# First loads reordered, a third q/k buffer and a VectorE norm for the last two tiles, in a linear-attention and FP4 feed-forward block

## The chip, the cores and the metric

The program runs on one core of one Trainium2 chip. The metric is the device time in microseconds (us) of one execution; for the kernel before, three runs gave 818.48, 820.93 and 820.97 us, so the median is 820.93 us. Lower is better. One further execution was recorded by the hardware profiler; all traces quoted here come from that one.

## What is computed

The input is x of shape (16, 512, 256). It goes through one transformer block, cut here to what matters:

```python
q, k = favor(split_heads(x @ Wq + bq)), favor(split_heads(x @ Wk + bk))   # softmax over 16 elements
v = split_heads(x @ Wv + bv)                                              # 16 heads of 16
attn = (q @ k.T / (sum(q) + EPS)) @ v @ Wo + bo
x = layernorm(x + attn)
h = silu(fp4(x) @ fp4(w_gate).T) * (fp4(x) @ fp4(w_up).T)                 # 704 wide
x = layernorm(x + fp4(h) @ fp4(w_down).T)
```

`fp4` quantises in blocks of 16 elements to the E2M1 grid with one scale a block and gives back f32 values. All matmuls are f32. The kernel uses that (q k^T) v equals q (k^T v), so no 512 x 512 matrix is formed.

## The kernel before, in words

The 16 batches have four tiles of 128 rows each; two tiles make a pair, so there are 32 pairs. For a batch, `load_x` (L373) brings x in one 512 KB DMA on SP's queue; `project` (L709), once a pair, transposes x on TensorE (`transposed`, L610, tile xT, copied out of PSUM by ScalarE at L620), multiplies by Wq and Wk (L724) and Wv (L734), adds the biases on VectorE (L727, L740), takes group maxima (L746) and subtracts them on GpSimd (L750). `features` (L754), once a batch, does exp on ScalarE (L761), sums on VectorE (L763), reciprocals (L774) and the scaling on GpSimd (L780). `key_values` (L784) forms k^T v (L793), masks it and multiplies by Wo (L807) into M. `attend` (L819), once a pair, transposes q (L617), multiplies by M (L835), and calls `norm`; the result x1n is written to DRAM.

`quantise` (L850), once a pair, reads x1 back from DRAM (L853, on SP's queue), finds FP4 codes (`codes`, L623: L635, L639 to L648), transposes them by a DMA (L864), spreads the scales by a PE transpose and a way through DRAM (L657 to L666), and multiplies both on GpSimd (L869) into xqT. `gate_up` (L873) does 32 matmul instructions of 352 columns (L889), SiLU (L894), the product (L896), FP4 codes again, a transposing DMA (L928) and the product on GpSimd (L932). `down` (L936) does 24 matmul instructions of 256 columns (L946), and `norm` with x1 as the residual; y goes out on ScalarE's queue (L957). For the last pair `down` calls `norm` for each tile by itself (L953), so that `us` holds one tile.

`norm` (L670): VectorE adds the residual and accumulates the row sum (L678); ScalarE takes the negative mean (L685) and the sum of squares (L687); GpSimd works out variance, the power -0.5 and the shift (L691 to L693); ScalarE applies them (L700).

The FFN's weights are quantised by the exact form of FP4 on the chip itself, in 8 chunks for gate and up and 4 for down (`weight_scales` L467, `fp4_exact` L506): some eight VectorE instructions a chunk, after one reduction over the whole of the raw weights (L477) and a row of scale arithmetic (L491 to L501). Their transposes (L562, L600) must be done before the first gate_up and the first down.

What sets the order: every piece of work is an `op` with an engine, an estimated time, a due time and its inputs and outputs. `Plan.order` (L145) is a list scheduler run on the host: over and over it takes, of each engine, the op that can start earliest (within 0.02 us the one due first), with the estimated end of its inputs plus 0.3 us, and the buffer that it needs must be free. The instructions are written out in that order, and each engine and DMA queue then runs its own in order on the chip. The estimates of the first loads are part of this: `DMA:x0` 6.0 us, `wqkv` 7.0, `wo` 14.0, `wgu` 13.0, `wdn` 16.0 (L377, L418 to L421). A `buf(shape, tag, n, name)` is one of n rotating buffers; an op that needs the n+1st waits until the first one's last reader is done. Counts that matter here: x 4 (L374), qk 2 (L713), v 2, x1 8 (`X1`, L315), x1n 3 (L842), xq 3 (L859, holds both xn and sqx).

The first loads are written out ahead of the plan in `load_all` (L425): x of batch 0 on SP's queue, then Wq, Wk, Wv on ScalarE's queue with bq, bk, bv on SP's, then w_gate, w_up and w_down, their big parts on ScalarE's queue (L440, L444) and two 64 KB tails on SP's (L443). SP follows with x of batch 1, then Wo and bo (`load_wo`, L446), and x of batches 2 and 3.

Of the kernel before, what the change touches and what calls it, by code (L numbers as in the profile page):

```python
# [13 lines left out]
ALU = mybir.AluOpType  # L14
AX = mybir.AxisListType

P = 128
# [11 lines left out]
LN_EPS = 1e-5  # L29
# [221 lines left out]
def t_dve(n):  # L251
    return 0.15 + n / 960.0
# [15 lines left out]
def tile_favor_fp4_block(  # L268
# [16 lines left out]
    nc = tc.nc  # L285
    B, L, D = hidden.shape
    FF = w_gate.shape[0]
    TPB = L // P
    PPB = TPB // 2
# [3 lines left out]
    D2, D3 = 2 * D, 3 * D  # L293
# [18 lines left out]

    NFF = 6

    X1 = 8  # L315
    plan = Plan()
    op = plan.op

    def buf(shape, tag, bufs, name, dtype=F32):
        return Buf(sb, [P] + list(shape), tag, bufs, name, dtype)  # L320
# [45 lines left out]
    def pu(ap):  # L366

        return ap.rearrange("p (u d) -> p u d", u=2)
# [3 lines left out]

    def load_x(b, due):  # L373
        x = buf([TPB, D], "x", 4, f"x_{b}")  # L374
        op("SP", 0.1, due, lambda: nc.sync.dma_start(x.tile, hidden[b].rearrange("(t p) d -> p t d", p=P)),
           outs=[x])
        op(f"DMA:x{b}" if b < 4 else "DMA", (6.0, 9.0, 16.0, 18.0, 3.5)[min(b, 4)], due, lambda: None, outs=[x])  # L377
        if b == 1:
            op("SP", 0.1, due, load_wo)
        xs[b] = x  # L380

    w_qkv = const.tile([P, DC, D3], F32, name="w_qkv")
# [1 line left out]
    w_o = const.tile([P, DC, D], F32, name="w_o")  # L384
    b_o = const.tile([P, D], F32, name="b_o")
    ident = const.tile([P, P], F32, name="ident")
    neg_half = const.tile([P, 2], F32, name="neg_half")
# [14 lines left out]
    gu_b, dn_b = big("wgu"), big("wdn")  # L402
    gu_flat = lambda: gu_b.tile.rearrange("p a b -> p (a b)")
    gu_rows = lambda: gu_flat().rearrange("p (c k) -> p c k", k=D)
    dn_flat = lambda: dn_b[:, 0, :]
    dn_rows = lambda: dn_flat().rearrange("p (c k) -> p c k", k=FF)
# [10 lines left out]

    wqkv_in, wo_in = (loaded(n, t) for n, t in (("wqkv", 7.0), ("wo", 14.0)))  # L418
    NGU, NDN = NW * D // F2, DC * FF // F2
    op("DMA:wgu", 13.0, 0.0, lambda: None, outs=[(gu_b, k) for k in range(NGU)])  # L420
    op("DMA:wdn", 16.0, 0.0, lambda: None, outs=[(dn_b, k) for k in range(NDN)])  # L421
    wguT_b = [Fixed(f"wguT{i}") for i in range(2)]
    wdT_b = Fixed("wdT")

    def load_all():  # L425

        gu_b.make()
        dn_b.make()
        gu_raw, dn_raw = gu_rows(), dn_rows()
        head = [o for o in plan.ops if o.eng == "SP"][:1]  # L430
        for o in head:
            for b in o.new:
                b.make()
            o.fn()
            o.fn = lambda: None
        for i, (w, bias) in enumerate(((Wq, bq), (Wk, bk), (Wv, bv))):
            nc.scalar.dma_start(w_qkv[:, :, i * D : (i + 1) * D], w.rearrange("(c p) n -> p c n", p=P))
            nc.sync.dma_start(b_qkv[:, i * D : (i + 1) * D], bias.partition_broadcast(P))
        for i, w in enumerate((w_gate, w_up)):
            nc.scalar.dma_start(  # L440
                gu_raw[:, i * NR : (i + 1) * NR, :], w[: NR * P].rearrange("(c p) k -> p c k", p=P)
            )
            nc.sync.dma_start(gu_raw[i * TR : (i + 1) * TR, 2 * NR, :], w[NR * P :])  # L443
        nc.scalar.dma_start(dn_raw, w_down.rearrange("(c p) k -> p c k", p=P))  # L444

    def load_wo():  # L446
        nc.sync.dma_start(w_o, Wo.rearrange("(c p) n -> p c n", p=P))
        nc.sync.dma_start(b_o, bo.partition_broadcast(P))

    def fill():  # L450
        make_identity(nc, ident)
# [218 lines left out]
    def norm(pr, add, dst, name, due, ins, r, junk, us=range(2)):  # L670

        n = len(us)
        key = None if n == 2 else us[0]
        rs, nm, var, rstd, nb = (buf([n], t if n == 2 else t + "1", 3, f"{t}_{name}") for t in ("rs", "nm", "var", "rstd", "nb"))

        def total():
            for k, u in enumerate(us):
                nc.vector.scalar_tensor_tensor(  # L678
                    r[:, u, :], pu(pr.tile)[:, u, :], 1.0, add(u), ALU.mult, ALU.add, accum_out=rs[:, k : k + 1]
                )  # L680

        op("DVE", n * (t_dve(D) + 0.06), due, total, ins=[(pr, key)] + ins, outs=[(r, key), rs])

        def square():
            nc.scalar.activation(nm.tile, rs.tile, AF.Identity, scale=-1.0 / D)  # L685
            for k, u in enumerate(us):
                nc.scalar.activation(junk(u), r[:, u, :], AF.Square, bias=nm[:, k : k + 1],  # L687
                                     accum_out=var[:, k : k + 1])

        def root():  # L690
            nc.gpsimd.tensor_scalar(var.tile, var.tile, 1.0 / D, LN_EPS, ALU.mult, ALU.add)  # L691
            nc.gpsimd.tensor_tensor(rstd.tile, var.tile, neg_half[:, :n], ALU.pow)
            nc.gpsimd.tensor_tensor(nb.tile, nm.tile, rstd.tile, ALU.mult)  # L693

        op("ACT", 0.35 + 0.6 * n, due, square, ins=[(r, key), rs], outs=[(dst, key), var, nm])
        op("POOL", 1.1, due, root, ins=[nm], outs=[var, rstd, nb])

        def apply():
            for k, u in enumerate(us):
                nc.scalar.activation(  # L700
                    dst[:, u, :], r[:, u, :], AF.Identity, bias=nb[:, k : k + 1], scale=rstd[:, k : k + 1]
                )

        op("ACT", 0.6 * n, due, apply, ins=[(r, key), nb, rstd], outs=[(dst, key)])


    qks, vs, Ms = {}, {}, {}

    def project(b, p, due):  # L709

        n = f"{b}_{p}"
        if p == 0:
            qks[b] = buf([TPB, D2], "qk", 2, f"qk_{b}")  # L713
            vs[b] = buf([TPB, D], "v", 2, f"v_{b}")
        x, qk, v = xs[b], qks[b], vs[b]
        xT = transposed(
            lambda: [x[:, 2 * p + u, c * P : (c + 1) * P] for u in range(2) for c in range(DC)],
            "xT", f"xT_{n}", due, [x],
        )
        for u in range(2):  # L720
            t = 2 * p + u
            pqk = psum("pm", f"pqk_{n}_{u}")
            for c in range(DC):
                op("PE", t_pe(D2), due, lambda c=c, u=u, pqk=pqk: nc.tensor.matmul(  # L724
                    pqk.tile, xT[:, 2 * u + c, :], w_qkv[:, c, :D2], start=c == 0, stop=c == DC - 1
                ), ins=[xT, wqkv_in], outs=[pqk], holds=[qk])
            op("DVE", t_dve(D2), due, lambda t=t, pqk=pqk: nc.vector.tensor_tensor(  # L727
                qk[:, t, :], pqk.tile, b_qkv[:, :D2], ALU.add), ins=[pqk], outs=[(qk, t)])
        pv = psum("pm", f"pv_{n}")

        def mm_v():
            for u in range(2):
                for c in range(DC):
                    nc.tensor.matmul(  # L734
                        pv[:, u * D : (u + 1) * D], xT[:, 2 * u + c, :], w_qkv[:, c, D2:],
                        start=c == 0, stop=c == DC - 1,
                    )

        op("PE", 2 * DC * t_pe(D), due, mm_v, ins=[xT, wqkv_in], outs=[pv], holds=[v])
        op("DVE", t_dve(2 * D), due, lambda: nc.vector.tensor_tensor(  # L740
            v[:, 2 * p : 2 * p + 2, :], pu(pv.tile), twice(b_qkv[:, D2:]), ALU.add
        ), ins=[pv], outs=[(v, p)])
        G = 2 * 2 * H
        mx = buf([G], "mx", 3, f"mx_{n}")
        qk3 = lambda: qk[:, 2 * p : 2 * p + 2, :].rearrange("p u (g e) -> p (u g) e", e=HD)
        op("DVE", t_dve(2 * D2), due, lambda: nc.vector.tensor_reduce(mx.tile, qk3(), AX.X, ALU.max),  # L746
           ins=[(qk, 2 * p), (qk, 2 * p + 1)], outs=[mx])
        for u in range(2):
            g = slice(u * 2 * H, (u + 1) * 2 * H)
            op("POOL", t_pool(D2), due, lambda g=g: nc.gpsimd.tensor_tensor(  # L750
                qk3()[:, g, :], qk3()[:, g, :], bcast(mx[:, g], HD), ALU.subtract
            ), ins=[mx], outs=[(qk, 2 * p + u)])
# [64 lines left out]
    st = {}  # L817

    def attend(b, p, due):  # L819
        i = b * PPB + p  # L820
        two = slice(2 * p, 2 * p + 2)
        x, qk, M = xs[b], qks[b], Ms[b]
# [6 lines left out]
           ins=[x, wo_in], outs=[xb])  # L829
# [9 lines left out]

        r = buf([2, D], "r1", 2, f"r1_{i}")  # L840
        op("PE", 2 * DC * t_pe(D), due, mm_a, ins=[qT, M], outs=[pa], holds=[r, xb], name="attend")
        x1 = buf([2, D], "x1n", 3, f"x1n_{i}")  # L842
        norm(pa, lambda u: xb[:, u, :], x1, f"a{i}", due, [xb], r, lambda u: x1[:, u, :])

        d = Buf(dr, [P, 2, D], "x1", NP, f"dx1_{i}")
# [4 lines left out]
    def quantise(i, due):  # L850
        x1 = st[i]["x1"] = buf([2, D], "x1", X1, f"x1_{i}")
        d = st[i]["d"]
# [3 lines left out]
        flat = lambda b: b.tile.rearrange("p u d -> p (u d)")  # L856
        am, iv = (small(n // BLK, t + "x", f"{t}_x{i}") for t in ("am", "iv"))
        scales = am, buf([n // BLK], "nsx", 2, f"ns_x{i}"), iv
        xn, sq = (buf([2, D], "xq", 3, f"{t}_{i}") for t in ("xn", "sqx"))  # L859
        xc = buf([n], "xc", 2, f"xc_{i}", U16)  # L860
        codes((lambda: flat(x1), x1), (lambda: flat(xn), xn), (lambda: flat(sq), sq), xc, 0, n, scales, 0,
              f"x{i}", due)
# [174 lines left out]
```

## Time and profile before

| what | value |
|---|---|
| median of three runs | 820.93 us |
| the profiled execution's own time | 821.11 us |
| its span, first to last instruction | 818.9 us |
| TensorE (PE) busy, matmul instructions | 786.8 us (96%), 3246 |
| VectorE (DVE) busy | 611.6 us (75%) |
| ScalarE (ACT) busy | 412.3 us (50%) |
| GpSimd (POOL) busy | 417.7 us (51%) |
| first matmul of the projections (L724) starts | 11.62 us |
| first gate_up matmul (L889) starts | 258.02 us |
| last matmul ends, last DMA issued | 812.6 us, 816.14 us |

The span is what lies between the first and the last instruction of the profiled execution; 2.2 us of its own time lie outside it. Engine rows count busy time; a busy TensorE can still run at half rate, so matmul counts times columns are the surer measure. In timeline rows the first number is the start in us, the second the length of the merged row, "x8" the number of instructions in it, and the bracket the idle time of that engine before the row with what ended it; ACTq and SPq are the DMA-issuing queues of ScalarE and SP.

### The profile page before, as it was taken

Reading aid. Unit: us, or ns where it says so; the run is one execution under the profiler, and the core shown is the slowest. Engines: PE = TensorE matmul, PEld = TensorE weight load, DVE = VectorE, ACT = ScalarE, POOL = GpSimd, SP = SyncE. Lnnn points to the kernel's source line nnn. Section 1 sums busy time; section 2 is a strip of 40 time slices with the busy share of each in tenths; the row PEclk is TensorE's granted clock in tenths of the full one; section 3 lists DMA queues with packets and bytes.
Section 4 is the critical chain, followed back from the end, with each engine's and each line's share of the span. In section 5 each row is a group of like instructions: output and inputs, shape, how many; then the busy total and the mean of one; then the engine's idle time right before and its main releaser. Section 6 shows DMA issues by size and latency. Waiting matters only on the chain.

```text
span 818.9 us, 10331 instructions
## 1 busy us (share of the span) xinstructions
PE 786.8 (96%) x3246; PEld 568.3 (69%) x3246; DVE 611.6 (75%) x1200; ACT 412.3 (50%) x924; POOL 417.7 (51%) x513
## 2 busy tenths in 40 slices
PE   5889998999999999999999999999999999999996
PEld 3566676767776767777777677777767777677674
DVE  1998998998888888668766765767767677675562
ACT  1245665745776563536563654544444444444433
POOL 0478786869888564536463534333333324333331
PEclk9989998999999999999999999999999999999999
DMA  8102241303012437766646564779797797886431
GB/s 280 32 0 93 89 146 31 109 2 104 27 38 79 88 65 150 124 100 107 112 102 100 106 123 115 127 147 144 123 148 135 145 141 131 147 131 126 119 76 38
DMA packets 104683, 85.98 MB, mean 105 GB/s; under 512 B 65037, under 2 KB 88117, under 8 KB 104629
## 3 DMA queue, kind: packets, MB, share of 16 engines
q1 hardware_dynamic: 84680, 63.81, 42.5%
q10 hardware_dynamic: 19949, 21.52, 9.4%
q8 instruction: 25, 0.41, 0.2%
q14 instruction: 29, 0.24, 0.1%
HBM read 51.25 MB, written 18.70 MB: 85 GB/s over the span
## 4 chain that ended last, share of the span: by engine, by line
PE 85%; DVE 8%; DMA 2%; POOL 2%; ACT 2%; issue 1%; SPq 0%; ACTq 0%; POOLq 0%; DVEq 0%
PE bank L889 36%; PE bank L946 20%; PE bank L724 11%; PE bank L835 6%; PE bank L734 5%; PE bank L793 3%; PE bank L617 2%; PE bank L807 2%; POOL qk L780 1%; DMA x<-dx 1%; DMA b_qkv<-in_L_attn_bk_dram 1%; DVE mx L746 1%; PE bank L657 1%; DVE qk L727 1%; DVE fs L763 1%
## 5 line engine op out<-in xcount | busy, mean ns | idle before, releaser
L889 PE MATMUL bank<-w_guT,xqT 128*128 128x352 f32 x1024 | 310.3, 459 | 0.0
L889 PEld LDWEIGHTS bank<-w_guT,xqT 128*128 128x128 f32 x1024 | 194.2, 190 | 101.4 <-issue 0.7
L946 PE MATMUL bank<-w_dT,hq 128*128 128x256 f32 x768 | 174.8, 380 | 0.6 <-DVE r L678 0.6
L932 POOL TENSOR_TENSOR hq<-hcT,hq 128x768 f32<-128x768 bf16 (+1 forms) x62 | 94.1, 1539 | 136.5 <-DMA hq<-d_h 117.3
L946 PEld LDWEIGHTS bank<-w_dT,hq 128*128 128x128 f32 x768 | 142.1, 190 | 24.9 <-issue 3.9
L896 DVE TENSOR_TENSOR h<-bank,g 128x352 f32<-128x352 f32 x128 | 66.3, 521 | 94.6 <-PE bank L889 53.9
L724 PE MATMUL bank<-w_qkv,xT 128*128 128x512 f32 x256 | 120.6, 606 | 4.5 <-ACT xT L620 4.5
L894 ACT ACTIVATE g<-bank 128x352 f32<-128x352 f32 x128 | 58.6, 460 | 122.3 <-PE bank L889 120.3
L750 POOL TENSOR_TENSOR qk<-qk,mx 128x512 f32<-128x512 f32 x64 | 70.4, 1119 | 33.2 <-DVE mx L746 33.2
L724 PEld LDWEIGHTS bank<-w_qkv,xT 128*128 128x128 f32 x256 | 48.5, 195 | 48.6 <-issue 39.2
L780 POOL TENSOR_TENSOR qk<-qk,fr 128x512 f32<-128x512 f32 x64 | 66.6, 1067 | 26.4 <-DVE fr L774 26.4
L646 ACT ACTIVATE sq<-h,magic 128x704 f32<-128x704 uint16 x64 | 56.4, 882 | 38.5 <-DVE h L643 37.6
L734 PE MATMUL bank<-w_qkv,xT 128*128 128x256 f32 x256 | 61.8, 385 | 0.0
L691 POOL TENSOR_SCALAR var_d<-var_d 128x2 f32<-128x2 f32 (+1 forms) x33 | 6.3, 191 | 108.1 <-ACT y L687 107.9
L727 DVE TENSOR_TENSOR qk<-bank,b_qkv 128x512 f32<-128x512 f32 x64 | 42.8, 682 | 24.9 <-PE bank L724 24.8
L835 PE MATMUL bank<-M,qT 128*128 128x256 f32 x256 | 59.6, 380 | 1.0 <-ACT xT L620 0.7
L734 PEld LDWEIGHTS bank<-w_qkv,xT 128*128 128x128 f32 x256 | 48.7, 194 | 14.5 <-issue 6.9
L635 DVE TENSOR_REDUCE bank<-h 128x44 f32<-128x704 f32 x64 | 57.2, 894 | 2.0
L643 DVE SCALAR_TENSOR_TENSOR h<-h,bank 128x704 f32<-128x704 f32 x64 | 56.7, 886 | 2.0
L835 PEld LDWEIGHTS bank<-M,qT 128*128 128x128 f32 x256 | 48.2, 190 | 13.1 <-issue 4.1
L648 DVE TENSOR_SCALAR hc<-sq 128x704 uint16<-128x704 uint16 x64 | 40.8, 640 | 16.2 <-ACT sq L646 16.1
L828 POOL TENSOR_TENSOR xb<-x,b_o 128x512 f32<-128x512 f32 x32 | 42.0, 1315 | 18.9 <-DVE r L678 15.4
(128 smaller groups left out, 1075.3 us busy)
## 6 DMA issues: line engine op xcount, KB each, us to landing
hq<-d_h SPq DMA_DIRECT2D x31, 704.0 KB
x<-_attn_hidden_states_dram SPq DMA_DIRECT2D x16, 512.0 KB
dx<-x1n ACTq DMA_DIRECT2D x32, 256.0 KB
x<-dx SPq DMA_DIRECT2D x32, 256.0 KB
xs<-d_x SPq DMA_DIRECT2D x32, 256.0 KB
out_dram<-y ACTq DMA_DIRECT2D x31, 256.0 KB
d_h<-sT_h ACTq DMA_DIRECT2D x31, 44.0 KB
wdn<-in_L_ffn_w_down_dram ACTq DMA_DIRECT2D x1, 704.0 KB
```

What stands on the lines that cost most here:

```text
L635: op("DVE", t_dve(n), due, lambda: nc.vector.tensor_reduce(amax[:, g], b3(src()), AX.X, ALU.max, apply_absolute_value=True), ins=[src_b], ...
L643: op("DVE", t_dve(n), due, lambda: nc.vector.scalar_tensor_tensor(b3(xn()), b3(src()), TIE * UP / BIG, bcast(inv[:, g], BLK), ALU.mult, AL ...
L724: op("PE", t_pe(D2), due, lambda c=c, u=u, pqk=pqk: nc.tensor.matmul(pqk.tile, xT[:, 2 * u + c, :], w_qkv[:, c, :D2], start=c == 0, stop=c ...
L734: nc.tensor.matmul(pv[:, u * D : (u + 1) * D], xT[:, 2 * u + c, :], w_qkv[:, c, D2:], start=c == 0, stop=c == DC - 1,)
L750: op("POOL", t_pool(D2), due, lambda g=g: nc.gpsimd.tensor_tensor(qk3()[:, g, :], qk3()[:, g, :], bcast(mx[:, g], HD), ALU.subtract), ins= ...
L780: nc.gpsimd.tensor_tensor(f3, f3, bcast(r[:, t * 2 * H : (t + 1) * 2 * H], HD), ALU.mult)
L835: nc.tensor.matmul(pu(pa.tile)[:, u, :], qT[:, 2 * u + c, :], M[:, c, :], start=c == 0, stop=c == DC - 1,)
L889: op("PE", t_pe(F2), due + u * 0.2 * PAIR, lambda c=c, u=u, lo=lo, ps_=ps_: nc.tensor.matmul(ps_[:, :F2], xqT[:, 2 * u + c, :], w_guT[:, c ...
L894: op("ACT", t_act(F2), due, lambda g=g, pg=pg: nc.scalar.activation(g.tile, pg[:, :F2], AF.Silu), ins=[pg], outs=[g], table="silu")
L896: op("DVE", t_dve(F2), due, lambda g=g, h=h, pu_=pu_, k=k: nc.vector.tensor_tensor(h[:, k * F2 : (k + 1) * F2], pu_[:, :F2], g.tile, ALU.m ...
L932: op("POOL", t_pool((gs.stop - gs.start) * P), d, lambda gs=gs: nc.gpsimd.tensor_tensor(part(1)[:, gs, :], hcT[:, gs, :], part(0)[:, gs, : ...
L946: op("PE", t_pe(D), due, lambda f=f, g=g, u=u: nc.tensor.matmul(pu(pd.tile)[:, u, :], part(1)[:, g, :], w_dT[:, f + u * (f == NR), :], sta ...
```

## The change

- x of batch 0 is loaded in two DMAs of 256 KB, one a pair, and the plan lets each pair's transposes wait for its own half only; the estimates are 4.5 and 5.5 us in place of 6.0.
- w_gate, w_up and w_down are no longer issued by ScalarE ahead of everything; SP issues all of their five DMAs after x of batch 1, Wo and bo (`load_rest`). The plan's estimates for them go from 13.0 to 16.0 and from 16.0 to 20.0 us.
- The last pair's two single-tile norms use VectorE: add, `bn_stats`, `bn_aggr`, add of epsilon; GpSimd takes the power; VectorE applies mean and factor.
- qk has 3 buffers in place of 2; x1 6 in place of 8, x1n 2 in place of 3, xq 2 in place of 3.

```diff
-    X1 = 8
+    X1 = 6
...
+        rows = hidden[b].rearrange("(t p) d -> p t d", p=P)
+        if b:
+            op("SP", 0.1, due, lambda: nc.sync.dma_start(x.tile, rows), outs=[x])
+            op(f"DMA:x{b}" if b < 4 else "DMA", (0, 9.0, 16.0, 18.0, 3.5)[min(b, 4)], due, lambda: None, outs=[x])
+        else:
+
+            def halves():
+                for p in range(PPB):
+                    nc.sync.dma_start(x[:, 2 * p : 2 * p + 2, :], rows[:, 2 * p : 2 * p + 2, :])
+
+            op("SP", 0.1, due, halves, outs=[x])
+            for p in range(PPB):
+                op(f"DMA:x{b}{p}", 4.5 + p, due, lambda: None, outs=[(x, p)])
         if b == 1:
-            op("SP", 0.1, due, load_wo)
+            op("SP", 0.1, due, load_rest)
...
-    op("DMA:wgu", 13.0, 0.0, lambda: None, outs=[(gu_b, k) for k in range(NGU)])
-    op("DMA:wdn", 16.0, 0.0, lambda: None, outs=[(dn_b, k) for k in range(NDN)])
+    op("DMA:wgu", 16.0, 0.0, lambda: None, outs=[(gu_b, k) for k in range(NGU)])
+    op("DMA:wdn", 20.0, 0.0, lambda: None, outs=[(dn_b, k) for k in range(NDN)])
...
+    def load_rest():
+        nc.sync.dma_start(w_o, Wo.rearrange("(c p) n -> p c n", p=P))
+        nc.sync.dma_start(b_o, bo.partition_broadcast(P))
+        gu_b.make()
+        dn_b.make()
+        gu_raw, dn_raw = gu_rows(), dn_rows()
         for i, w in enumerate((w_gate, w_up)):
-            nc.scalar.dma_start(
+            nc.sync.dma_start(
                 gu_raw[:, i * NR : (i + 1) * NR, :], w[: NR * P].rearrange("(c p) k -> p c k", p=P)
             )
             nc.sync.dma_start(gu_raw[i * TR : (i + 1) * TR, 2 * NR, :], w[NR * P :])
-        nc.scalar.dma_start(dn_raw, w_down.rearrange("(c p) k -> p c k", p=P))
...
+        nc.sync.dma_start(dn_raw, w_down.rearrange("(c p) k -> p c k", p=P))
...
+        if n == 1:
+            u = us[0]
+            rstd = buf([1], "rstd1", 2, f"rstd_{name}")
+            st, mv = buf([6], "st1", 2, f"st_{name}"), buf([2], "mv1", 2, f"mv_{name}")
+
+            def stats():
+                nc.vector.tensor_tensor(r[:, u, :], pu(pr.tile)[:, u, :], add(u), ALU.add)
+                nc.vector.bn_stats(st.tile, r[:, u, :])
+                nc.vector.bn_aggr(mv.tile, st.tile)
+                nc.vector.tensor_scalar(mv[:, 1:2], mv[:, 1:2], LN_EPS, None, ALU.add)
+
+            op("DVE", 2 * t_dve(D) + 0.1, due, stats, ins=[(pr, key)] + ins, outs=[(r, key), st, mv])
+            op("POOL", 0.7, due, lambda: nc.gpsimd.tensor_tensor(rstd.tile, mv[:, 1:2], neg_half[:, :1], ALU.pow), ins=[mv], outs=[rstd])
+            op("DVE", t_dve(D), due, lambda: nc.vector.tensor_scalar(
+                dst[:, u, :], r[:, u, :], mv[:, 0:1], rstd[:, 0:1], ALU.subtract, ALU.mult),
+               ins=[(r, key), mv, rstd], outs=[(dst, key)], port=True)
+            return
...
-            qks[b] = buf([TPB, D2], "qk", 2, f"qk_{b}")
+            qks[b] = buf([TPB, D2], "qk", 3, f"qk_{b}")
...
-            "xT", f"xT_{n}", due, [x],
+            "xT", f"xT_{n}", due, [x if b else (x, p)],
...
-        x1 = buf([2, D], "x1n", 3, f"x1n_{i}")
+        x1 = buf([2, D], "x1n", 2, f"x1n_{i}")
...
-        xn, sq = (buf([2, D], "xq", 3, f"{t}_{i}") for t in ("xn", "sqx"))
+        xn, sq = (buf([2, D], "xq", 2, f"{t}_{i}") for t in ("xn", "sqx"))
```

More of the change, by code (lines that the diff above doesn't have):

```diff
@@ L374, in load_x @@
         x = buf([TPB, D], "x", 4, f"x_{b}")
-        op("SP", 0.1, due, lambda: nc.sync.dma_start(x.tile, hidden[b].rearrange("(t p) d -> p t d", p=P)),
-           outs=[x])
-        op(f"DMA:x{b}" if b < 4 else "DMA", (6.0, 9.0, 16.0, 18.0, 3.5)[min(b, 4)], due, lambda: None, outs=[x])
+        rows = hidden[b].rearrange("(t p) d -> p t d", p=P)
[9 more added lines that the diff above has]
+                op(f"DMA:x{b}{p}", 4.5 + p, due, lambda: None, outs=[(x, p)])
         if b == 1:
-            op("SP", 0.1, due, load_wo)
+            op("SP", 0.1, due, load_rest)
         xs[b] = x
@@ L425, in load_all @@
     def load_all():
-        gu_b.make()
-        dn_b.make()
-        gu_raw, dn_raw = gu_rows(), dn_rows()
         head = [o for o in plan.ops if o.eng == "SP"][:1]
@@ L443, in load_all @@
             nc.sync.dma_start(gu_raw[i * TR : (i + 1) * TR, 2 * NR, :], w[NR * P :])
[L444 to L448, printed above, removed]
+        nc.sync.dma_start(dn_raw, w_down.rearrange("(c p) k -> p c k", p=P))
     def fill():
@@ L673, in norm @@
         key = None if n == 2 else us[0]
-        rs, nm, var, rstd, nb = (buf([n], t if n == 2 else t + "1", 3, f"{t}_{name}") for t in ("rs", "nm", "var", "rstd", "nb"))
+        if n == 1:
[13 more added lines that the diff above has]
+            return
+        rs, nm, var, rstd, nb = (buf([n], t, 3, f"{t}_{name}") for t in ("rs", "nm", "var", "rstd", "nb"))
         def total():
```

## The prediction, made before the changed kernel was run

> **What bounds the kernel now.** I read the page's engine rows, then the table of busy time by 20 us stages, then the timeline of the stages that are not full. TensorE is busy 96% of the span, but how full is a stage really? Where nothing stalls, 32 matmuls of 352 columns take 9.47 us, so a column costs 0.83 ns. Matmul counts by stage times columns times 0.83 ns give the work done; the rest of the stage is lost.
>
> ```profile
> 20.00:40.00 20.00, 17.36 (x64) 10.54 (x62) 19.43 (x29) 5.62 (x8) 9.48 (x9) 1.00 0.12 37
> 40.00:60.00 20.00, 15.44 (x62) 11.60 (x63) 19.02 (x36) 8.34 (x16) 13.23 (x14) 0.83 0.00 0
> ...
> 100.00:120.00 20.00, 20.00 (x87) 14.03 (x86) 19.36 (x34) 12.60 (x30) 17.56 (x23) 1.00 0.41 127
> 120.00:140.00 20.00, 17.23 (x75) 13.73 (x74) 17.64 (x33) 10.44 (x20) 11.90 (x14) 0.83 0.20 62
> ```
>
> The columns are busy PE, PE weight load, DVE, ACT, POOL, then clock. Lost time, so counted: 13.6 us in 0:20, 2.9 in 20:40, 8.1 in 40:60, 6.6 in 120:140, 2.5 in 160:180, 1.0 in 220:240, 1.4 in 500:540, some 3 over 540:800, 7.6 in 800:819, and nearly nothing elsewhere, together close to the 56 us between the span and 763 us of pure matmul. From 180 to 800 TensorE is the bound; a microsecond won before 180 and not lost again comes off the end. VectorE, at 19.4 of 20 us in 20:40, is the second limit there.
>
> The start, from the timeline:
>
> ```profile
> 5.67 1.94 PE L617 MATMUL bank<-ident,x 128*128 128x128 f32 x8 [5.67 <-DMA x<-_attn_hidden_states_dram]
> ...
> 9.28 0.38 ACTq L444 DMA_DIRECT2D wdn<-in_L_ffn_w_down_dram  x1
> 9.68 1.28 ACT L620 ACT_TABLE_LOAD   x1 [9.68 <-DMA b_qkv<-in_L_attn_bk_dram]
> 10.98 1.07 ACT L620 COPY xT<-bank 128x512 f32<-128x512 f32 x2
> ...
> 11.62 6.52 PE L724 MATMUL bank<-w_qkv,xT 128*128 128x512 f32 x8 [4.01 <-ACT xT L620]
> ```
>
> ScalarE issues the FFN loads, and its queue stands in them (issues at 2.41, 6.49, 9.28 us) until 9.66; only then come its table load and the copy of xT that L724 waits for, though the transposes ended at 7.6. The middle:
>
> ```profile
> 36.62 1.04 PE L617 MATMUL bank<-ident,x 128*128 128x128 f32 x8
> 37.61 2.28 DVE L763 TENSOR_REDUCE fs<-qk 128x128 f32<-128x2048 f32 x1
> ...
> 41.35 4.11 POOL L780 TENSOR_TENSOR qk<-qk,fr 128x512 f32<-128x512 f32 x4 [2.15 <-DVE fr L774]
> ...
> 42.46 0.69 PE L617 MATMUL bank<-ident,qk 128*128 128x128 f32 x2 [4.81 <-POOL qk L780]
> ```
>
> Batch 2's x is transposed at 36.62, yet its first L724 runs at 50.09: both qk buffers are held until batch 0's q is transposed at 47.8. Meanwhile PE waits 4.81 us and comes back at half rate (ten L793 in some 2.5 us, against 16 in 1.8 later). 121.38 to 134.68 has the same picture. The end:
>
> ```profile
> 812.64 0.42 DVE L678 SCALAR_TENSOR_TENSOR r<-bank,x 128x256 f32<-128x256 f32 x1 [2.52 <-PE bank L946]
> ...
> 813.46 0.20 ACT L685 ACTIVATE nm_d<-rs_d 128x1 f32<-128x1 f32 x1 [0.43 <-DVE r L678]
> ...
> 814.66 0.55 POOL L692 TENSOR_TENSOR rstd_d<-var_d,neg_half 128x1 f32<-128x1 f32 x1
> ...
> 815.51 0.60 ACT L700 ACTIVATE y<-r,nb_d,rstd_d 128x256 f32<-128x256 f32 x1 [1.22 <-POOL nb_d L693]
> 816.14 0.35 ACTq L957 DMA_DIRECT2D out_dram<-y  x1
> ```
>
> From the last matmul to the last DMA issue: 3.5 us, over three engines.
>
> **Head: -4.2 us.** Without FFN issues ScalarE is free at 2.4 and its 1.28 us table load is over by 3.7 (that such a load does not wait for its copy's data shows at 258.31, where one runs while L889 still computes). By 4.0 us some 0.53 MB had landed, shared by x and Wq, so x's first 256 KB is there near 4.1 where all 512 KB took until 5.5. Four transposes at the cold pace (1.94/8 x 4 = 1.0 us) and a copy of 0.56 give xT at about 6.1. Then L724 waits for Wk: SP's wait for that load ends at 7.15. So L724 starts near 7.4, not 11.62. If it waited for the whole of w_qkv (Wv, 9.9) the gain would be 1.5; both ends stay in the range. The bias for L727 (bk, 9.3) is there before its first matmuls end (7.4 + 3.4).
> Two rules bear on this. The Trainium skill, "DMA: Bandwidth & Descriptors", section "Issuing engines are not separate DMA queues", says that loads from either queue share the same 16 engines and a second issuer saves only issue time. By it the move to SP is worth three issues, 0.38 + 0.38 + 0.49 = 1.2 us. The row says that ScalarE stood for 7 us because its issues waited for earlier loads to land; I take the row. The second, "TensorE: Matmul & The Clock Gate", "What's actually happening", has the array at half rate until busy for some 3.4 us. Here L724 ran at 0.85 us instead of 0.43 for over 6 us. With transposes at 4.4 and no long gap the rule would end the slow stretch at 8 to 11 and win up to 1.5 us more (four matmuls); the row wins nothing. I take the row, and keep 1.5 for the lower bound.
> On SP's queue Wo, bo, five FFN loads and x of batches 2 and 3 now stand in line. Before, 5.7 MB kept the engines full until 20.5 us; the bytes are the same. x, Wqkv, biases, batch 1, Wo, bo and gate/up make 4.0 MB, so gate/up lands near 15 instead of 13; its first reader L477 ran at 20.63. Batches 2 and 3 land at 20.5, needed at 36.6; SP's next work is at 66. Cost: nothing, at most 1 us if x of batch 2 were late in a start moved up by 10.
>
> **Third qk: -6 us in 20:60, -3 us in 120:180.** Batch 2's 16 L724 instructions (16 x 0.43 = 6.8 us) can run in the hole after 37.7, without v, and PE keeps its clock: lost there are 11.0 us, so at most 9 come back (6.8 plus 2 of half rate). Against it: their L727 (4 x 0.68) and L746 (2 x 1.21), 5.1 us, come earlier on a VectorE that is 97% busy, ahead of batch 0's sums. L763 already ran at 37.61 though exp ended at 31.05, since weight arithmetic and other batches stood before it; with gate/up planned at 16 instead of 13 that block falls behind more of the projections, which helps. Bounds 0 and -9, taken -6. In 120:140 and 160:180 9.1 us are lost the same way; VectorE is 88 to 93% busy there and PE would arrive 10 us sooner with the same weight work to carry, so I take a third, bounds +3 and -9. X1 = 6 also moves the codes of pairs 6 and 7 (two of the four L635 that ran at 126.6 to 130.9, in that very stall) behind the first downs at 314, where VectorE has 5 us free in 20. If the weight chunks slip, PE has attention work until 513, so that costs nothing.
>
> **Tail: -1.1 us.** New chain after the last matmul: add 0.42 (L678's row), bn_stats: no row; nearest is L635, 0.68 for 512, so 0.42 for 256, at worst 0.68; bn_aggr and the add of epsilon 0.20 each (L639's row), gaps 0.1: 1.35. Power 0.55 after 0.1. Apply in f32 from SBUF: L648 has 0.53 for 704, so 0.3, at worst 0.42, plus 0.05. Sum 2.35 against 3.47, and ScalarE no longer waits behind the other tile's issue. Between -0.6 and -1.4; taken -1.1. The other tile is hidden: PE works until 812.6.
>
> **Fewer x1, x1n, xq: +2.5 us.** No row shows the shorter rings. x1n: attends of the same parity are 17 us apart early, its write lasts a few; free. xq: one quantise per 14.87 us; free. x1: before, the ninth read waits for down 0's L678 (314.14, issue at 314.94); now the seventh does. A read takes 7 to 10 us (issue 499.29, L635 runs on it at 509.15). The plan thinks 3.5, so VectorE now and then stalls: 9.2 us in 4 stalls, one of which cost PE 1.3 us at 512.22. I allow two more of these, 2.5; bounds 0 and 6.
>
> **Sum.** -4.2 - 6 - 3 - 1.1 + 2.5 = -11.8 against a span of 818.9 and an own time of 821.11, so 809.3; the median is 0.2 lower: 809 us.
>
> **Rivals.** (a) The middle gives its gain back: PE runs ahead, but VectorE at 97% only moves the hole to the next batch. Then head, tail and part of x1's cost remain: -3 to -6, 815 to 818. For it: L763's 6.5 us behind other work. Against: 16 L724 stood ready in the hole. (b) All of it comes back and the clock warms early: -4.2 - 1.5 - 9 - 5 - 1.1 = -20.8, 800. For it: PE fully used after 180 needs only stored work. (c) Slower: the x1 loop becomes the bound. x1 of pair k+6 is read after down k. Read to L869: 9.9, codes and queue up to the transposing DMA 12.6 (509.15 to 521.79), the DMA and the product some 8.5: 31 us, an estimate from these rows; gate_up to its L678: 769.04 to 806.62, 37.6. Loop 69 us against six periods of 14.87, 89.2. It decides from a chain of 51 us; at 58 the loop is 95.6, 1.1 us a pair over some 19 pairs, +20, so about 830. Against it: 20 us of slack. (d) The halves and the third buffer do nothing, because w_qkv is waited for whole and VectorE binds: within 2 us.
>
> **Chances.** -7 to -16 (the forecast) 0.52; (a) 0.17; (b) 0.11; (c) 0.12; (d) 0.08. A measurement of this kernel can tell about 0.3%, 2.5 us, from no change. Faster 0.80, same 0.08, slower 0.12. Range 801 to 819: it leaves out (c) and the tail of (b).
>
> **What would show it.** ACT's first copy near 5.5 and L724 near 7.4; L724 of batch 2 directly behind batch 1's and no 4.8 us wait before the first q transposes; lost time in 20:60 below 5 us and in 120:180 below 6; no L700 after the last matmul, last issue 2.4 us behind it; period 14.87 unchanged. Wrong if gate_up waits for L869 after 314, if L724 starts at 10, or if the holes reappear before 180.

## The result and the profile after

In 19 runs each the changed kernel has a median of 816.79 us (811.22 to 819.58) and the kernel before 819.58 us (818.48 to 821.50): ratio 0.9953, 95% interval 0.9937 to 0.9969, so 3.9 us faster, 2.5 to 5.2 (the two medians alone differ by 2.8). Forecast were 11.8. The time lies in the range and in that of rival (a), at a third of the forecast gain.

The profiled execution took 812.95 us (span 810.9), 3.8 less than the median of its kernel, while that of the kernel before took 821.11, 1.5 more than its median: of the 8.0 us between the two spans, some 5 come from which executions were recorded. Its busy time by stages, columns as before:

```profile
0.00:20.00 20.00, 15.20 (x50) 9.35 (x51) 7.34 (x9) 3.53 (x5) 7.76 (x19) 1.00 0.89 265
20.00:40.00 20.00, 20.00 (x85) 13.20 (x84) 19.59 (x33) 5.08 (x6) 9.53 (x10) 1.00 0.17 54
...
120.00:140.00 20.00, 19.98 (x98) 14.69 (x97) 18.76 (x33) 14.27 (x30) 17.48 (x23) 1.00 0.20 68
...
260.00:500.00 240.00, 232.20 (x940) 165.49 (x940) 170.45 (x337) 123.82 (x273) 112.36 (x134) 0.99 0.53 104
```

PE is now full in 20:40 and nearly so in 120:140, two of the stages that had the holes. But 260:500 has 7.8 us without PE work, where the kernel before was busy throughout (20.00 of 20 in every stage). Counted as in the prediction (matmuls times columns times 1/1200 us, the prediction's 0.83 ns, against the stage), the lost time is:

| stage, us | before | after | change | forecast |
|---|---|---|---|---|
| 0:20 | 13.6 | 7.2 | -6.4 | -4.2 |
| 20:180 | 23.5 | 10.5 | -13.0 | -9 |
| 180:540 | 6.4 | 19.0 | +12.6 | +2.5 |
| after the last matmul (span's end) | 6.3 | 5.3 | -1.0 | -1.1 |

These add up to -7.8, against -8.0 between the two spans. Of the +12.6 in 180:540, 7.9 are idle time of TensorE (9.75 us in place of 1.87); half-rate stretches behind the waits are in the rest. The head, from the timeline:

```profile
2.38 1.28 ACT L630 ACT_TABLE_LOAD   x1 [2.38 <-issue]
...
4.27 1.08 PE L627 MATMUL bank<-ident,x 128*128 128x128 f32 x4 [4.27 <-DMA x<-_attn_hidden_states_dram]
...
5.39 0.59 ACT L630 COPY xT<-bank 128x512 f32<-128x512 f32 x1 [1.73 <-PE bank L627]
...
6.50 4.70 PE L751 MATMUL bank<-w_qkv,xT 128*128 128x512 f32 x8
```

L751 is the old L724. It starts at 6.50 instead of 11.62, and its first eight take 4.70 us instead of 6.52: the half-rate stretch is shorter. The old hole at 37.7:

```profile
30.56 2.74 PE L751 MATMUL bank<-w_qkv,xT 128*128 128x512 f32 x6
33.13 0.60 PE L627 MATMUL bank<-ident,qk 128*128 128x128 f32 x4
33.57 1.88 PE L751 MATMUL bank<-w_qkv,xT 128*128 128x512 f32 x4
35.29 1.95 PE L820 MATMUL bank<-qk,v 128*128 128x128 f32 x16
```

Batch 2's projections now run before the first q transposes, which wait for nothing, and k^T v (L820) runs at full rate. The end:

```profile
805.60 0.42 DVE L690 TENSOR_TENSOR r<-bank,x 128x256 f32<-128x256 f32 x1 [1.65 <-PE bank L973]
806.06 0.43 DVE L691 BATCH_NORM_STATS2 st_d<-r 128x6 f32<-128x256 f32 x1
806.52 0.18 DVE L692 BATCH_NORM_AGGREGATE mv_d<-st_d 128x2 f32<-128x6 f32 x1
...
807.56 0.42 DVE L697 TENSOR_SCALAR y<-r,mv_d,rstd_d 128x256 f32<-128x256 f32 x1 [0.23 <-POOL rstd_d L696]
```

2.4 us from the add to the end of the apply, as forecast (2.35). And a stall that the kernel before did not have:

```profile
261.27 2.27 DVE L790 TENSOR_REDUCE fs<-qk 128x128 f32<-128x2048 f32 x1
...
264.94 3.09 POOL L807 TENSOR_TENSOR qk<-qk,fr 128x512 f32<-128x512 f32 x3 [2.33 <-DVE fr L801]
...
266.05 0.44 PE L627 MATMUL bank<-ident,qk 128*128 128x128 f32 x2 [2.81 <-POOL qk L807]
...
267.45 5.30 PE L751 MATMUL bank<-w_qkv,xT 128*128 128x512 f32 x8
```

It is the hole of 42.46 again, 220 us later: sums on VectorE, scaling on GpSimd, then TensorE, which waits 2.81 us and comes back slow (5.30 us for eight L751, 3.60 at full rate). Another kind of stall begins with a read of x1 that has not landed when VectorE wants it:

```profile
485.82 0.69 DVE L645 TENSOR_REDUCE bank<-x 128x32 f32<-128x512 f32 x1 [3.68 <-DMA x<-dx]
...
488.16 0.31 PE L667 MATMUL bank<-ident,ns_h 128*88 128x128 f32 x1 [1.45 <-DVE ns_h L649]
```

VectorE stands 3.68 us, the scales of h (L649) come late by that, and TensorE waits 1.45 us for them.

### The profile page after: what moved, and what is told of

It reads as the page before. It is cut to its first block, busy times and chain, and to the rows that moved or that the text cites. A ratio compares the mean times of both kernels' runs of the same rounds, so it can differ in the third digit from the quotient of the medians.

```text
span 810.9 us, 10314 instructions
## 1 busy us (share of the span) xinstructions
PE 782.8 (97%) x3246; PEld 561.9 (69%) x3246; DVE 611.6 (75%) x1206; ACT 410.7 (51%) x916; POOL 418.9 (52%) x509
## 4 chain that ended last, share of the span: by engine, by line
PE 75%; DVE 9%; DMA 7%; ACT 3%; POOL 2%; issue 2%; SPq 0%; ACTq 0%; POOLq 0%; DVEq 0%
PE bank L916 31%; PE bank L973 18%; PE bank L751 10%; PE bank L862 5%; PE bank L761 4%; DMA x<-dx 4%; PE bank L820 3%; PE bank L627 2%; POOL qk L807 1%; PE bank L834 1%; DMA w_qkv<-in_L_attn_Wv_dram 1%; DMA xcT<-xc 1%; DMA wgu<-in_L_ffn_w_up_dram 1%; DVE fs L790 1%; PE bank L667 1%
## 5 line engine op out<-in xcount | busy, mean ns | idle before, releaser
L751 PE MATMUL bank<-w_qkv,xT 128*128 128x512 f32 x256 | 121.6, 608 | 5.1 <-ACT xT L630 5.0
L777 POOL TENSOR_TENSOR qk<-qk,mx 128x512 f32<-128x512 f32 x64 | 68.3, 1090 | 35.4 <-DVE mx L773 35.4
L751 PEld LDWEIGHTS bank<-w_qkv,xT 128*128 128x128 f32 x256 | 47.3, 195 | 48.4 <-issue 39.3
L718 POOL TENSOR_SCALAR var_d<-var_d 128x2 f32<-128x2 f32 x31 | 5.9, 191 | 113.5 <-ACT y L714 113.2
L761 PEld LDWEIGHTS bank<-w_qkv,xT 128*128 128x128 f32 x256 | 48.0, 190 | 14.8 <-issue 8.1
L896 POOL TENSOR_TENSOR xqT<-xcT,xs 128x512 f32<-128x512 bf16 x32 | 37.7, 1178 | 29.4 <-DMA xs<-d_x 21.4
```

The source lines that it names most:

```text
L761: nc.tensor.matmul(pv[:, u * D : (u + 1) * D], xT[:, 2 * u + c, :], w_qkv[:, c, D2:], start=c == 0, stop=c == DC - 1,)
```

## The experiments

Theory R: the shorter x1 ring makes the new waits. Theory V: VectorE and GpSimd are full, so what TensorE wins it waits for later. Theory O, formed after the first four runs: the list scheduler draws a new order whenever an estimate or a buffer count changes, and the order of before is a good draw that the change throws away. Each ratio is taken against runs of the kernel before on the same chip (medians 819.3 to 820.0). Lost times come from one profiled execution of each kernel.

**X1 back at 8.**

```diff
-    X1 = 6
+    X1 = 8
```

> The changed kernel with X1 back at 8 (qk 3, x1n 2, xq 2, new loads and new last norms stay). Theory R (the shorter x1 ring makes the new waits of TensorE after 180 us, some 14 us of lost time in the changed kernel's trace): lost time over 180:540 falls from 14 to under 5 us and the time from 816.8 to 806 to 810. Theory V (VectorE and GpSimd are full until 300 us, so that TensorE, 15 us ahead after the head and the third qk, only meets the same wait later): lost time over 180:540 stays at 10 to 16 us and the time within 3 us of 816.8.

814.46 us, ratio to before 0.9938 (0.9919 to 0.9958), which overlaps that of the changed kernel. Lost over 180:540: 19.2 us, where R wanted under 5. VectorE's waits for x1 fell from 19.9 us in 9 stalls to 12.6 in 6, yet 10.5 us are now lost in 220:260, one wait of 5.4 us for M among them. R falls, as far as one order can tell (this edit too makes a new one): the ring makes some of VectorE's stalls, but the loss stays without it. V's time came true, its loss of 10 to 16 us did not.

**qk back at 2.**

```diff
-            qks[b] = buf([TPB, D2], "qk", 3, f"qk_{b}")
+            qks[b] = buf([TPB, D2], "qk", 2, f"qk_{b}")
```

> The changed kernel with qk back at 2 buffers (rings 6, 2, 2, new loads, new last norms stay). If the third qk is worth what the trace of the changed kernel shows in 20:180 (some 15 us) and none of the later waits come from it (theory R): 826 to 832. If the later waits are the same microseconds moved (theory V): 814 to 819, with 8 to 15 us lost in 20:180 again and under 6 us in 180:540.

828.62 us, 1.0113 (1.0098 to 1.0129): slower than both kernels. Lost in 20:180 28.4 us, in 180:540 15.5. V in its plain form (the same microseconds, moved) falls. The time lies in R's range; but R's reason for more than the 819.6 of before was the x1 ring, and the last run speaks against that. So none of the theories explains why the rest of the change is *slower than before*.

**The loads as before, the rest changed.** On the changed kernel; x's halves and the two pairs' inputs go back likewise.

```diff
-            op("SP", 0.1, due, load_rest)
+            op("SP", 0.1, due, load_wo)
...
-    op("DMA:wgu", 16.0, 0.0, lambda: None, outs=[(gu_b, k) for k in range(NGU)])
-    op("DMA:wdn", 20.0, 0.0, lambda: None, outs=[(dn_b, k) for k in range(NDN)])
+    op("DMA:wgu", 13.0, 0.0, lambda: None, outs=[(gu_b, k) for k in range(NGU)])
+    op("DMA:wdn", 16.0, 0.0, lambda: None, outs=[(dn_b, k) for k in range(NDN)])
...
         for i, w in enumerate((w_gate, w_up)):
-            nc.sync.dma_start(
+            nc.scalar.dma_start(
...
-        nc.sync.dma_start(dn_raw, w_down.rearrange("(c p) k -> p c k", p=P))
+        nc.scalar.dma_start(dn_raw, w_down.rearrange("(c p) k -> p c k", p=P))
```

> The changed kernel with the loads, their queues and their estimates as before (qk 3, rings 6, 2, 2, new last norms stay). The first L724 is back at 11.6 us. If the head's gain reaches the end (prediction: 4.2 us, trace: 6.4 us in 0:20): 821 to 823. Theory V: the head's gain is eaten by VectorE before 300 us, so within 2 us of the changed kernel's 816.8.

822.41 us, 1.0027 (1.0015 to 1.0039). The loads are worth 5.6 us in this surrounding, as if the head's gain reached the end. The sum alone does not show that it did: the order is a new one here too, and the trace loses 17.3 us in 20:180 (10.5 with the new loads) and 17.2 in 180:540 (19.0).

**Only the loads changed.** The load part of the change on the kernel before, the reverse of the last edit; two of its lines:

```diff
-            op("SP", 0.1, due, load_wo)
+            op("SP", 0.1, due, load_rest)
...
-            "xT", f"xT_{n}", due, [x],
+            "xT", f"xT_{n}", due, [x if b else (x, p)],
```

> The kernel before with only the new loads, their queues and estimates. If the head's gain reaches the end: 819.6 - 6.4 = 813 (812 to 815), with lost time of 0:20 at 7.2 us. Theory V: VectorE holds TensorE back, the hole at 38 to 50 us and that at 121 to 134 grow by what the head won, and the time is 817 to 820.

825.19 us, 1.0084 (1.0057 to 1.0111): both were wrong, by 5 to 13 us. The head's loss fell to 8.1 us, but 33.7 us were lost in 20:180 (in a profiled execution of 832.39 us, 7.2 above the median, so part of this may be that execution's own). Loads alone make the kernel slower, third qk and rings without them also; together they make it faster. That does not add up, unless something else changes in each: the order. The next four runs test that.

**New loads, old order.** The DMAs of the change, but the plan keeps x's 6.0, 13.0 and 16.0 and lets both pairs wait for all of x; the compute instructions of PE, VectorE, ScalarE and GpSimd then stand in the order of before, one for one.

```diff
-            for p in range(PPB):
-                op(f"DMA:x{b}{p}", 4.5 + p, due, lambda: None, outs=[(x, p)])
+            op(f"DMA:x{b}", 6.0, due, lambda: None, outs=[x])
...
-    op("DMA:wgu", 16.0, 0.0, lambda: None, outs=[(gu_b, k) for k in range(NGU)])
-    op("DMA:wdn", 20.0, 0.0, lambda: None, outs=[(dn_b, k) for k in range(NDN)])
+    op("DMA:wgu", 13.0, 0.0, lambda: None, outs=[(gu_b, k) for k in range(NGU)])
+    op("DMA:wdn", 16.0, 0.0, lambda: None, outs=[(dn_b, k) for k in range(NDN)])
```

> The kernel before with the new first loads as DMAs, but with the old estimates in the plan, so that PE, VectorE, GpSimd and, its three DMA issues aside, ScalarE have instruction for instruction the order of before. Theory O (what the loads alone lost, 825.2 against 819.5, is the new order that the estimates bring, not the loads): the head's gain reaches the end, 813 to 815. Theory V (VectorE is full and returns the head's gain whatever the order): 818 to 821, with more lost than before at 33 to 46 and 116 to 130 us.

818.83 us, 0.9988 (0.9979 to 0.9997): 1.0 us faster, which is V's range. 6.8 us less are lost in 0:20, 6.4 more in 20:40. The reduction over gate and up before (L477), then in this run (L486), and here the first q transposes:

```profile
20.63 3.07 DVE L477 TENSOR_REDUCE wdn<-wgu 128x176 f32<-128x2816 f32 x1
...
18.68 3.09 DVE L486 TENSOR_REDUCE wdn<-wgu 128x176 f32<-128x2816 f32 x1 [5.16 <-DMA wgu<-in_L_ffn_w_up_dram]
...
40.20 0.69 PE L626 MATMUL bank<-ident,qk 128*128 128x128 f32 x2 [6.95 <-POOL qk L789]
```

But V's reason does not hold: VectorE is not full, it stands 5.16 us before the reduction, since up had not landed. It starts only 1.95 us sooner than before, and the q transposes only 2.26 (42.46 before).

**Old loads, new order.** The kernel before with the new estimates alone, and each pair of batch 0 waiting in the plan for its own half of x.

```diff
-        op(f"DMA:x{b}" if b < 4 else "DMA", (6.0, 9.0, 16.0, 18.0, 3.5)[min(b, 4)], due, lambda: None, outs=[x])
+        if b:
+            op(f"DMA:x{b}" if b < 4 else "DMA", (0, 9.0, 16.0, 18.0, 3.5)[min(b, 4)], due, lambda: None, outs=[x])
+        else:
+            for p in range(PPB):
+                op(f"DMA:x{b}{p}", 4.5 + p, due, lambda: None, outs=[(x, p)])
...
-    op("DMA:wgu", 13.0, 0.0, lambda: None, outs=[(gu_b, k) for k in range(NGU)])
-    op("DMA:wdn", 16.0, 0.0, lambda: None, outs=[(dn_b, k) for k in range(NDN)])
+    op("DMA:wgu", 16.0, 0.0, lambda: None, outs=[(gu_b, k) for k in range(NGU)])
+    op("DMA:wdn", 20.0, 0.0, lambda: None, outs=[(dn_b, k) for k in range(NDN)])
...
-            "xT", f"xT_{n}", due, [x],
+            "xT", f"xT_{n}", due, [x if b else (x, p)],
```

> The kernel before with the new estimates in the plan only: the order of the loads-only kernel, instruction for instruction, while the DMAs are issued as before. Theory O: the order alone costs what the loads-only kernel lost plus the head's gain, so 829 to 833. Theory V: the order costs little, 818 to 822.

833.12 us, 1.0149 (1.0128 to 1.0171), as O said: a few entries of the plan that no engine and no DMA ever sees cost 12 us. From its timeline:

```profile
82.94 0.55 PE L621 MATMUL bank<-ident,qk 128*128 128x128 f32 x2 [3.44 <-ACT sT_x L663]
84.24 0.69 PE L621 MATMUL bank<-ident,qk 128*128 128x128 f32 x2 [0.74 <-POOL qk L784]
90.01 0.37 PE L661 MATMUL bank<-ident,ns_x 128*32 128x128 f32 x1 [5.08 <-DVE ns_x L643]
```

PE, which takes its work in the written order, stands 5.08 us at a scale transpose (L661) that VectorE has not prepared. k^T v comes behind it at 90.18, though the scaling of q and k that it needs (L784) was done at 86.7.

**Redrawn orders of both kernels.** Each edit changes one number that only the plan reads: the estimate of gate and up (`wgu`), or `LAG`, the allowance between engines. The diffs show one of each; the other values (15.0 in place of 13.0, and 0.29) stand in the same lines.

```diff
-LAG = 0.3
+LAG = 0.31
```

```diff
-    op("DMA:wgu", 16.0, 0.0, lambda: None, outs=[(gu_b, k) for k in range(NGU)])
+    op("DMA:wgu", 15.0, 0.0, lambda: None, outs=[(gu_b, k) for k in range(NGU)])
```

> The changed kernel with the estimate of one load, gate and up, at 15.0 in place of 16.0 us: nothing that the chip does differs but the order. Theory O: the time moves by several us, up or down (between 808 and 830, more than 2 us from 816.8). Theory R or V: within 2 us of 816.8, since the buffers and the engines' load are the same.

> The kernel before with the plan's allowance between engines at 0.31 in place of 0.30 us: again nothing but the order differs, and no buffer or load is changed. Theory O (the order of before is a lucky one of many; a redrawn order costs several us in waits of TensorE): 822 to 832. Theory R or V: 819.5 within 2 us.

> The changed kernel with the plan's allowance between engines at 0.31 us: a second redrawn order of the changed kernel. Theory O (the time of any one order is a draw; the new buffers and loads shift the mean of the draws): 814 to 828, and lower than the redrawn orders of before (828.5 for this allowance). Theory R or V: 816.8 within 2 us.

> The kernel before with the allowance at 0.29 us: a second redrawn order of before. Theory O: 823 to 833, as the two redrawn orders so far (828.5 and 833.1). If those two were bad luck and the order of before is an ordinary one: 816 to 822.

> The changed kernel with the plan's allowance at 0.29 us: a third redrawn order of the changed kernel. If the buffers and loads are worth some 12 us against a redrawn order of before (theory O: 833 for this allowance): 814 to 827. If the changed kernel's own 816.8 and the 815.2 at 0.31 were luck and the mean of its orders is no better than that of before: 827 to 834.

> The kernel before with the estimate of gate and up at 15.0 in place of 13.0 us: a fourth redrawn order of before, by another knob than the allowance. Theory O: 823 to 834. If only the allowance spoils the order of before: 818 to 822.

| order | time, us | ratio to before (95%) | lost 20:180 | lost 180:540 |
|---|---|---|---|---|
| before, its own | 819.6 | 1 | 23.5 | 6.4 |
| before, LAG 0.31 | 828.53 | 1.0100 (1.0085 to 1.0114) | 27.6 | 11.0 |
| before, LAG 0.29 | 832.83 | 1.0160 (1.0138 to 1.0182) | 28.7 | 15.3 |
| before, wgu 15 | 825.60 | 1.0060 (1.0043 to 1.0078) | 27.0 | 9.4 |
| before, new estimates | 833.12 | 1.0149 (1.0128 to 1.0171) | 29.5 | 14.6 |
| after, its own | 816.79 | 0.9953 (0.9937 to 0.9969) | 10.5 | 19.0 |
| after, LAG 0.31 | 815.20 | 0.9947 (0.9933 to 0.9961) | 13.3 | 19.0 |
| after, LAG 0.29 | 826.95 | 1.0068 (1.0047 to 1.0089) | 17.5 | 26.0 |
| after, wgu 15 | 826.08 | 1.0068 (1.0049 to 1.0087) | 18.9 | 23.0 |

All four redrawn orders of before are 5 to 13 us slower than its own, by the ratios; their mean is 830.0. The changed kernel's four orders, its own among them, have a mean of 821.3; its three redrawn ones 822.7. The loss in 20:180 does not overlap between the kernels (27.0 to 29.5 against 10.5 to 18.9), and neither does that in 180:540 (9.4 to 15.3 against 19.0 to 26.0). So loads and buffers win some 13 us in 20:180 in every order tried (means 28.2 and 15.1), and some 9 are lost again after it (12.6 and 21.8). Two expectations do not decide: LAG 0.31 on the changed kernel lies within 2 us of its own time, so in the ranges of O and of R and V alike, and LAG 0.29 ends at the edge between its two ranges. With four draws each, spreads of 8 and 12 us, and the changed kernel's own order counted but not that of before, the difference of the means, 8.7 us, is uncertain by about as much (its standard error is 3.5 us).

Sorted by the number of qk buffers that the plan counts, all 17 traces of this document, those of the runs below included, fall into two groups. The six with three lose 10 to 19 us in 20:180 and 17 to 26 in 180:540; the eleven with two lose 22 to 34 and 6 to 16. Old loads with three buffers (17.3 and 17.2), eight x1 with three (10.1 and 19.2), and new loads and short rings with two (28.4 and 15.5) stay on their sides. So the move of the loss goes with the third qk in the plan, more than with the loads or the x1 ring. The last margin is small, and x1n and xq at 2 go with every plan of three; they were not tried apart.

**Gate and up first, old order; then with the new last norms.** The new loads in the order of before once more, but SP issues gate and up before batch 1's x, with w_down behind Wo and bo; the lines that move:

```diff
             nc.sync.dma_start(b_qkv[:, i * D : (i + 1) * D], bias.partition_broadcast(P))
+        gu_b.make()
+        dn_b.make()
+        gu_raw, dn_raw = gu_rows(), dn_rows()
+        for i, w in enumerate((w_gate, w_up)):
+            nc.sync.dma_start(
+                gu_raw[:, i * NR : (i + 1) * NR, :], w[: NR * P].rearrange("(c p) k -> p c k", p=P)
+            )
+            nc.sync.dma_start(gu_raw[i * TR : (i + 1) * TR, 2 * NR, :], w[NR * P :])
```

> The new first loads with the order of before, as in the run that gained 1.0 us, but with gate and up issued by SP right after the biases, ahead of x of batch 1, Wo and bo. Theory D (with the order held, the head's gain was given back because VectorE stood 5.2 us at its reduction over gate and up, which landed only at 18.7 us): that reduction starts at 15.5 to 17, the first q transposes at 37 to 38.5 in place of 40.2, and the time is 815.5 to 817. Theory V (VectorE is full anyhow): within 1 us of 818.8.

814.19 us, 0.9931 (0.9918 to 0.9944): 5.7 us faster than before by the ratio, more than expected, and outside V's 1 us around 818.8. From its timeline:

```profile
15.17 3.09 DVE L486 TENSOR_REDUCE wdn<-wgu 128x176 f32<-128x2816 f32 x1 [0.19 <-DMA wgu<-in_L_ffn_w_up_dram]
...
36.73 0.69 PE L626 MATMUL bank<-ident,qk 128*128 128x128 f32 x2 [4.80 <-POOL qk L789]
```

The reduction is 5.46 us sooner than before, the q transposes 5.73, and that reaches the end. Then the same with the change's branch for one-tile norms:

```diff
+        if n == 1:
+            u = us[0]
...
+                nc.vector.tensor_tensor(r[:, u, :], pu(pr.tile)[:, u, :], add(u), ALU.add)
+                nc.vector.bn_stats(st.tile, r[:, u, :])
+                nc.vector.bn_aggr(mv.tile, st.tile)
...
+            return
```

> The same with the two last norms on VectorE: 1.0 us less than the run without them (0.6 to 1.4), whatever holds for the head; so 814.5 to 816 by theory D.

813.11 us, 0.9921 (0.9907 to 0.9934): the norms are worth 1.1 us by the medians, though the two ranges touch (813.75 to 814.38 and 812.92 to 814.18). Its interval lies below that of the changed kernel, and its median is the lowest here, without a third qk or a shorter ring.

**Three real qk buffers, the plan counts two.** On the run with gate and up first (814.19 us), so the order stays:

```diff
+HELD = {"qk": 3, "x1n": 2, "fs": 1}
...
-            self.tile = pool.tile(shape, self.dtype, tag=self.tag, name=name, bufs=self.bufs)
+            self.tile = pool.tile(shape, self.dtype, tag=self.tag, name=name, bufs=HELD.get(self.tag, self.bufs))
```

> The run with gate and up first (814.2 us), the order held, but with three real qk buffers while the plan counts two (paid for by x1n at 2 and the sums' buffer at 1, in the tiles only). Theory O: a third buffer that the order does not use is worth nothing, 813.7 to 815.5, and the first q transposes still wait 4.8 us. If it is the buffer itself, and not the order, that lets TensorE go on: 806 to 811.

814.51 us, 0.9928 (0.9910 to 0.9945), and the same wait at the same place:

```profile
36.45 0.69 PE L627 MATMUL bank<-ident,qk 128*128 128x128 f32 x2 [4.79 <-POOL qk L790]
```

In this order the buffer does nothing: TensorE takes its work as written, and batch 2's projections stand behind those transposes. It acts through the order that the plan makes of it.

## Why the prediction was right in its parts and wrong in its sum

**Head, -4.2: right, and more.** L724's successor starts at 6.50 (forecast 7.4), on Wq and Wk without Wv, and without the wait for Wk that the forecast had put at 7.15. Of the two rules weighed there, I took the row against the clock gate's; the rule was nearer. With TensorE busy from 4.27 on, the slow stretch ended after some 4.4 us (L751's weight loads come 0.86 us apart up to 8.21, 0.43 apart from 8.89 on), and eight matmuls took 4.70 us instead of 6.52: that is the 1.5 us kept for the lower bound, and more.

**"Cost: nothing" for the FFN loads on SP: wrong.** I put gate and up near 15 us by bytes. ScalarE's issue of up before (L440), then SP's queue after the change, where the loads of gate and up are L454 and L457:

```profile
6.49 0.38 ACTq L440 DMA_DIRECT2D wgu<-in_L_ffn_w_up_dram  x1
...
6.79 1.10 SPq L454 DMA_DIRECT2D wgu<-in_L_ffn_w_gate_dram  x1
10.85 0.58 SPq L457 DMA_DIRECT2D wgu<-in_L_ffn_w_gate_dram  x1
11.47 0.58 SPq L454 DMA_DIRECT2D wgu<-in_L_ffn_w_up_dram  x1
12.10 0.53 SPq L457 DMA_DIRECT2D wgu<-in_L_ffn_w_up_dram  x1
```

The standing that ScalarE was freed of is SP's now, from 7.9 to 10.85 us, and up goes out at 11.47 where it had gone at 6.49. With the order held, its landing at 18.7 cost 4.7 of the 5.7 us that the head can win. In the changed kernel the new order puts other work before that reduction, which starts at 18.96 without a wait, so there it cost little.

**Third qk, -9 in 20:180: right in kind, too small.** -13.0 in the trace, and redrawing the orders leaves that difference (28.2 and 15.1). That it works through the order was not in the prediction; it follows from the last experiment.

**Tail, -1.1: right,** -1.0 in the spans and 1.1 in the experiment.

**The step that failed:** "From 180 to 800 TensorE is the bound; a microsecond won before 180 and not lost again comes off the end", with the term of +2.5 us for what is lost later, put on the x1 ring. It measured +12.6, in an execution quicker than most. That nearly nothing was lost after 180 was a property of one order, not of the engines: redrawing the order of before, with no other edit, loses 9.4 to 15.3 us there instead of 6.4, and 3.5 to 6 more ahead of it. In all four redraws of before, the new order alone cost 5 to 13 us. Against redrawn orders, the change is worth an estimated 9 us, with the uncertainty above; against the one it replaced, 3.9.

Against the 12.6 us that the redrawn orders of before lose there on average, 6 (its own order, 19.0) to 9 us (the mean of its four, 21.8) belong to the change: all its orders lose 19 us or more after 180. Rival (a), for which I gave 0.17, had the time and half the mechanism: the gain comes back, though little of it at the next batches (60:100 lost 4.3 in place of 1.4) and most after 180, where feature chains (266.05) and x1 reads (488.16) stall it. That X1 alone makes the loss is not borne out: with eight it was 19.2. The sorting by qk points to the third qk, but how much it, the shorter rings and the earlier TensorE each make stays open, since each trial of one draws a new order. Rival (c) did not occur: the loss lies before 540, and 540:780 lost 1.1 us (before: 1.5).

The account of lost time had a fault as well, which is alike on both sides and leaves the differences standing. The losses listed add up to 46.7 us, not to 56: 9.47 us over 32 x 352 columns is 0.84 ns a column, so at 0.83 about 1% of the 763 us of full-rate work, some 7 us, is counted as lost and lies spread over the whole span.

Last, the sum of the trace (-7.8) is not the measured gain, since the profiled execution is 3.8 us quicker than the median; where a median execution loses these 3.8 us is not recorded. Over the 19 runs of the changed kernel the mean granted clock goes from 0.991 to 0.999 and the span falls by 0.93 us for each 0.001 (a straight line through the 19 pairs). Half rate alone would make it 0.81, an estimate (0.001 of 811 us), so the runs seem to differ in how long TensorE ran at half rate. That the short waits decide this is an inference.

## What to carry to other kernels

Where a scheduler orders the instructions, an edit of a buffer count or an estimate has two effects, the resource and a new order. Change one with the other held (the same order with other DMAs; the same DMAs with another order) and redraw the order of the kernel before a few times with neutral numbers, before a difference of 1% is put down to the resource; redraw the changed kernel as often. And when DMA issues move to another queue, look up which of them wait there for earlier ones to land, and who needs their data: here, putting the loads of gate and up ahead of batch 1's x, Wo and bo brought 4.7 us, about as much as the whole change.

## What was not expected of the hardware

One program, run 19 times, took 811.22 to 819.58 us, while the kernel before stayed within 818.48 to 821.50 in its 19 runs. The page "TensorE: Matmul & The Clock Gate" of the Trainium skill ("What's actually happening") says that the window which decides on the rate runs freely and is not tied to the program's start; that fits the first eight projections' 4.44, 4.70 and 5.60 us in three kernels which start them within 0.3 us of each other, but no run here shows the window itself.
